# Delta's copies ahead of delta u, a constant row on TensorE, and large transfers in pieces, in a four-layer state-space kernel

## The chip, the cores and the metric

One core of one Trainium2 chip runs the whole program. Its engines are TensorE (PE; PEld is its loading of weights), VectorE (DVE), ScalarE (ACT), GpSimd (POOL) and SyncE (SP). SP issues every DMA here. The metric is the device time of one execution in microseconds (us), lower being better; it is given as the median of three runs, beside one profiled execution.

## The reference

Four layers run on x of 8 x 48 x 48 x 96 numbers; each adds to x a selective scan over a depthwise convolution. Of layers 0 to 2 (B = 8 batches, L = 2304 positions, Din = 192 channels, N = 16 states, K = 4 directions), cut to what matters:

```
xc, z = split(groupnorm(x) @ in_proj_w.T);  xc = silu(depthwise_conv3x3(xc) + conv_b)
xs = stack([x_hw, x_wh, reversed x_hw, reversed x_wh])        # 4 directions
dts, Bs, Cs = split(einsum('bkdl,kcd->bkcl', xs, x_proj_w))   # the projection
delta = softplus(dt_proj_w @ dts + dt_proj_b);  A = -exp(A_logs)
for each position:                                            # the scan
    h = exp(delta * A) * h + (delta * u) * B                  # per channel, per state
    y = sum over states of h * C
y = sum of the 4 directions + D * u
x = x + (layernorm(y) * silu(z)) @ out_proj_w.T
```

Layer 3 writes the scan as decay * cumsum(delta * B * u / (decay + 1e-12)), with decay = exp(cumsum(delta * A)). That decay runs to zero within some positions.

## The kernel before

**Tiling.** The eight batches go through a layer two at a time ("pair"); layers 0 to 2 make 12 pairs. The 192 channels of the pair's two batches are three tiles t of 128 partitions: 128 channels of batch 0, 128 of batch 1, and the 64 left of both. A pair has 12 *groups* (t, phase ph, direction d): ph says along which image axis the positions run, d whether forward or backward. A group has three *chunks* of 768 positions (`SCAN`), and a chunk 16 *units* n. A unit holds two states of 64 channels on its 128 partitions, so 16 units make 16 states of 128 channels. That is 576 units a pair and 6912 in layers 0 to 2.

**One unit** does this. ACT makes the decay exp(delta * A) (`exp`, L764). For ten of the 16 units, PE spreads the rows of B from `brow` into PSUM (`spread_rows`, L667), DVE multiplies with delta u (`scan`, L794) and DVE scans (L798). For the other six, those of `pooled` (L712), DMA brings B already spread (`bb`, L724), POOL multiplies it with delta u ahead of time (`weigh`, L741), and the decay stands in PSUM. POOL then multiplies the scan's h by C (`cb`, loaded spread by DMA; L807), and PE sums over the states (`add_up`, L854) into `acc`, which ACT adds to y (`collect`, L871) at the end of a chunk.

**Order of the work.** `run` (L1170) writes the program's order by hand, one unit after the other, and each engine executes its own instructions in that order. Iteration k issues `get_ready(k + 1)`: loads of C three units ahead, of B four (`LOADS`), `weigh` and the decays two ahead (`DECAYS`), the spread of the next unit. Then comes unit k's scan and the sums of unit k - 2 (`LAG`). So the weighing for unit j stands on POOL just ahead of the product of unit j - 3. Since every DMA goes through SP in this order, a DMA that has to wait on SP for its data or buffer holds the DMAs behind it.

**Side work** is written as generators, and one `yield` is a step. `prepare` (L580) makes delta and delta u for the next chunk, one step a unit, in two halves of 384 positions. `prologue` (L287, the next pair: norm, projection, convolution, the projections xd of dts, B and C) and `epilogue` (L998, the pair before: layer norm, gate, output) get one step a unit between them, shared out by their planned totals of 300 and 195 steps (L1238, L1240).

**Delta** is softplus(v) = relu(v) + log(1 + e), with e = exp(-|v|) and a correction e - ((1 + e) - 1). A half issues three ACT instructions for |v|, relu and e (L611 to L613), three for log, w1 = 1 + e and then 1 - w1 (L615 to L617), and eight fp32 matmuls that add e, w1, log and relu into a PSUM bank v (L623). `to_twins` (L574, L578) then copies v by four ACT instructions of 64 partitions into `dl`, where each half of the channels stands twice. DVE multiplies v by u in place in PSUM (`times_u`, L631 and L634), and four more copies of L578 write delta u into `du`. Banks of `psum` are two, and the side work uses them too.

**Large transfers.** The prologue loads x of a batch whole (864 KB, L366; in layer 0 it stores it, L364), and stores the projection of a phase and batch whole (684 or 864 KB, L492). Four steps after the latter it reads B and C back (`raw`, L437), cuts them into three bf16 parts and stores those as `xb` (L456), from which `brow` is loaded (L749, with the chunk's first C). y of a tile is stored whole (1152 KB, L875), and the epilogue, whose first load is its first step, reads it back as `ey` (L1030).

**Layer 3** (`Edge`, L877) computes the two ends of the 2304 positions alone, 192 each, and tests that the decay has run out; the whole layer runs again under a condition otherwise. Its 48 chunks take the last tenth of the time.

Of the kernel before, what the change touches and what calls it, by code (L numbers as in the profile page):

```python
# [40 lines left out]
BF16 = mybir.dt.bfloat16  # L41
AF = mybir.ActivationFunctionType
# [61 lines left out]
def ss2d_layers_kernel(ctx: ExitStack, tc: tile.TileContext, x_in, consts, weights, out):  # L104
# [55 lines left out]
    nc.vector.tensor_copy(pick, sel[: 2 * NR])  # L160


    twin = cpool.tile([P, 64], F32, name="twin")
    nc.vector.tensor_add(twin, ident[:, 0:64], ident[:, 64:P])

# [14 lines left out]
    nc.vector.tensor_add(centre, ident, off)  # L180
    centre_22 = cpool.tile([P, P], F32, name="centre_22")
    nc.vector.tensor_add(centre_22, ident, off_22)
    minus_group = cpool.tile([DM, DM], F32, name="minus_group")
    nc.scalar.activation(minus_group, group_w, AF.Copy, scale=-1.0)

# [101 lines left out]
    def prologue(l, p, short=False, first=False):  # L287
# [44 lines left out]
        for b in range(2):  # L332
            x = tmp.tile([DM, L], F32, name=f"x_{l}_{p}_{b}", tag="tmp")
            if l == 0:
                loaded = []

                def load(c0, m):
                    ld = sm2.tile([P, 4, DM], F32, name="ld", tag="ld")
                    nc.sync.dma_start(
                        ld[: m // 4],  # L340
                        x_in[2 * p + b, c0 : c0 + m, :].rearrange("(q j) c -> q j c", j=4),
                    )
                    loaded.append(ld)

                load(*CHUNKS[0])
                load(*CHUNKS[1])
                for _ in range(3):
                    yield
                for i, (c0, m) in enumerate(CHUNKS):
                    q, ld = m // 4, loaded[i]  # L350
                    ps = bank()
                    for j in range(4):
                        nc.tensor.transpose(
                            ps[0:DM, j * q : (j + 1) * q], ld[:q, j, :], ident[:q, :q]
                        )
                    yield True
                    nc.scalar.copy(
                        x[:, c0 : c0 + m].rearrange("c (q j) -> c j q", j=4),
                        ps[0:DM, :m].rearrange("c (j q) -> c j q", j=4),
                    )  # L360
                    if i + 2 < NCH:
                        load(*CHUNKS[i + 2])
                    yield
                nc.sync.dma_start(src[b], x)  # L364
            else:
                nc.sync.dma_start(x, src[b])  # L366
            for _ in range(4):
                yield


# [57 lines left out]
        def later(i, held, f, *args):  # L428
            steps.setdefault(i, []).append((held, f, args))
# [37 lines left out]
        def x_projection(i, ph, b):  # L467

            o, got = 15 * i, {}

            def put(ps, c0, m):
                if "xt" not in got:
                    got["xt"] = tmp.tile([ly.nx, L], F32, name=f"xt_{l}_{p}_{ph}_{b}", tag="tmp")
                xt, r0, nr = got["xt"], c0 // W, m // W
                if ph == 0:
                    nc.scalar.copy(xt[:, c0 : c0 + m], ps[: ly.nx, :m])
                else:
                    nc.scalar.copy(
                        xt.rearrange("p (w h) -> p h w", h=H)[:, r0 : r0 + nr, :],
                        ps[: ly.nx, :m].rearrange("p (r w) -> p r w", w=W),  # L480
                    )

            def mul(half, c0, m):
                if half == 0:
                    got["ps"] = bank()
                project(got["ps"], ph, b, half, lambda z: z[:, c0 : c0 + m], slice(0, m))

            for j, (c0, m) in enumerate(CHUNKS):
                later(o + 3 * j, True, mul, 0, c0, m)
                later(o + 3 * j + 1, True, mul, 1, c0, m)  # L490
                later(o + 3 * j + 2, False, lambda *a: put(got["ps"], *a), c0, m)
            later(o + 15, False, lambda: nc.sync.dma_start(xd[ph, b], got["xt"]))  # L492
            row = 2 * ly.rank
            parts_of(
                o + 19, ph, b,
                lambda d: xd[ph, b, row + 2 * NS * d : row + 2 * NS * d + NS, :].rearrange(
                    "n (q m) -> (n q) m", q=4
                ),
                lambda d: xb[ph, b, :, d].rearrange("k n (q m) -> (n q) k m", q=4),
                4 * NS, L // 4,  # L500
            )
# [69 lines left out]
                state[c.l, c.p]["xd"][c.ph, b, c.d * r : (c.d + 1) * r, c.c0 : c.c0 + c.m],  # L571
            )

    def to_twins(z, at, v):  # L574

        for g in range(2):
            for h in range(2):
                nc.scalar.copy(z[64 * h : 64 * h + 64, g, at], v[64 * g : 64 * g + 64])  # L578

    def prepare(c):  # L580
        l, p, t, ph, d = c.l, c.p, c.t, c.ph, c.d
        ly, s = layers[l], state[l, p]
# [10 lines left out]
        for z in range(0, c.m, HALF):  # L593
# [23 lines left out]
            nc.scalar.activation(w1, w1, AF.Identity, bias=ones, scale=-1.0)  # L617
            yield
            v = bank()[:, :m]
            for i, z1 in enumerate((e, w1, lg, x)):  # L620
                for g in range(2):
                    half = slice(64 * g, 64 * g + 64)
                    nc.tensor.matmul(  # L623
                        v[half], ident[:, half], z1, start=(i == 0), stop=(i == 3)
                    )
                if i % 2 == 1:
                    yield

            def times_u(o):
                if ph == 0:  # L630
                    nc.vector.tensor_mul(o, v, u[:, c.c0 + z : c.c0 + z + m])  # L631
                    return
                r0 = (c.c0 + z) // H
                nc.vector.tensor_mul(  # L634
                    o.rearrange("p (w h) -> p w h", h=H),
                    v.rearrange("p (w h) -> p w h", h=H),
                    u[:, r0 : r0 + m // H, :],
                )
# [18 lines left out]
            yield  # L657


    def pieces(m):  # L660
# [8 lines left out]
                start=True, stop=True,  # L669
            )  # L670

    late_act, late_sums = [], []

    def collected():
        some = bool(late_sums)
# [8 lines left out]
    class Chunk:  # L684
# [23 lines left out]

        def pooled(self, n):

            return n in (2, 5, 7, 10, 13, 15) and self.l < NLAYER - 1

# [24 lines left out]
        def weigh(self, n):  # L737

            if self.pooled(n):
                b = self.b[n][:, : self.m]  # L740
                nc.gpsimd.tensor_mul(b, b, self.du[n % 2])  # L741

        def load(self, n):

            s, m, at = state[self.l, self.p], self.m, slice(self.c0, self.c0 + self.m)
            if n == 0:
                self.brow = rpool.tile([2 * NR, SCAN], BF16, name="brow", tag="brow")
                for j, b in enumerate(range(2) if self.t == 2 else (self.t, self.t)):
                    nc.sync.dma_start(  # L749
                        self.brow[NR * j : NR * j + NR, :m],  # L750
                        s["xb"][self.ph, b, :, self.d, :, at],
                    )
            self.cb[n] = cb = cbpool.tile([P, SCAN], F32, name="cb", tag="cb")
            self.fetch(cb, NS, n)

# [107 lines left out]
        def collect(self):  # L863

            l, p, t, s = self.l, self.p, self.t, state[self.l, self.p]
            if self.ph == self.d == 0 and self.first:
                s["y", t] = ypool.tile([P, L], F32, name=f"y_{l}_{p}_{t}", tag="y")
            acc = self.acc[:, :, : self.m // 2]
            if self.ph == 1:
                acc = acc.rearrange("p a (w h) -> p a w h", h=H)  # L870
            nc.scalar.copy(self.y_part(s["y", t]), acc)  # L871
            if self.ph == self.d == 1 and self.last:
                if t == 0:
                    s["yd"] = dram.tile([3, P, L], F32, name=f"yd_{l}_{p}", tag="yd")
                nc.sync.dma_start(s["yd"][t], s["y", t])  # L875

    class Edge:  # L877

# [119 lines left out]
    def epilogue(l, p):  # L998
# [26 lines left out]
        def load(i):  # L1025
# [144 lines left out]
    def run(pairs, short):  # L1170
# [58 lines left out]
        for k, ((l, p, unit), c, n) in enumerate(todo):  # L1229
# [172 lines left out]
```

## Time and profile before

| | |
|---|---|
| three runs | median 20515.53 us, 20514.31 to 20521.39 |
| the profiled execution's own time | 20509.65 us |
| its span, first to last instruction | 20507.7 us |
| TensorE clock granted, mean | 0.904 |
| busy over the span | POOL 87%, DVE 86%, PE 84%, ACT 79% |
| layers 0 to 2, 300 to 18550 us | POOL 16959 us of 18250, DVE 16669, PE 15470, ACT 14655 |
| layer 3, 18550 us to the end | PE 1592 us of 1958, ACT 1446, DVE 895, POOL 720 |
| DMA moved | 4200 MB, 221 GB/s at a busy share of 0.85 in layers 0 to 2 |

How to read it. A row of the groups names a line, an engine, an operation, what it writes and reads, the shape, the count, then busy us, mean ns of one, and the engine's idle time before those instructions with what ended it. A row of the waits says who waited for whom: total us, times, longest. A row of the windows gives a stretch (from:to and its length), then the busy us and the count of instructions for PE, PEld, DVE, ACT and POOL, then the granted clock, the busy share of the DMA engines and GB/s. A row of the timeline has start, length, engine, line, operation, out<-in, and in brackets the idle time before it and what ended that. SPq is SP issuing a DMA, not moving it.

### The profile page before, as it was taken

The numbers are of one execution on the slowest core, as the hardware profiler recorded it, in microseconds if no ns is written. First come the engines' busy times: TensorE is split into PE (matmuls) and PEld (weight loads), VectorE is DVE, ScalarE is ACT, GpSimd is POOL, SyncE is SP. The second block draws the span as 40 slices with busy tenths as digits, with TensorE's granted clock in tenths as the row PEclk, the third lists the DMA queues.
The fourth block names the chain that finished last, engine by engine and source line by source line (L and its number), as shares of the span: only waits on it lengthen the run. The fifth ranks groups of instructions, "written<-read, shape, count | busy, mean of one in ns | idle before, by whom it ended". The sixth has DMA issues, their size and how long they took to land. (4 is left out here: it accounts for less than half of the span.)

```text
span 20507.7 us, 304889 instructions
## 1 busy us (share of the span) xinstructions
PE 17283.2 (84%) x88322; PEld 7546.6 (37%) x88322; DVE 17656.0 (86%) x14161; ACT 16243.7 (79%) x30020; POOL 17768.2 (87%) x10121
## 2 busy tenths in 40 slices
PE   8888888888888888888888888888888888888886
PEld 2323333333333333333333333333333333335565
DVE  5999999999999999999999999989989989995543
ACT  5777887887887887887877887877877877877776
POOL 5999999999999999999999999999999999995432
PEclk8998998998998999998998999988988998999997
DMA  5888888888888888888888888888888888883221
GB/s 147 223 221 222 219 220 224 222 219 221 220 225 222 219 229 221 221 229 219 221 228 220 217 225 219 218 218 220 217 219 219 220 219 222 219 220 109 76 72 51
DMA packets 1963444, 4200.13 MB, mean 205 GB/s; under 512 B 369456, under 2 KB 720048, under 8 KB 1948592
## 3 DMA queue, kind: packets, MB, share of 16 engines
q1 hardware_dynamic: 1961776, 4180.52, 77.8%
q8 instruction: 726, 11.89, 0.3%
q14 instruction: 942, 7.72, 0.2%
HBM read 4026.64 MB, written 152.27 MB: 204 GB/s over the span
## 5 line engine op out<-in xcount | busy, mean ns | idle before, releaser
L807 POOL TENSOR_TENSOR cb<-cb,da 128x768 f32<-128x768 f32 x4320 | 7831.3, 1817 | 799.5 <-issue 258.3
L854 PE MATMUL acc<-cb,twin 128*64 128x384 f32 x27648 | 7018.1, 542 | 663.6 <-POOL cb L807 660.3
L798 DVE TENSOR_TENSOR_SCAN da<-da,carry,b 128x768 f32<-128x768 f32 x2880 | 5223.3, 1814 | 176.4 <-ACT b L764 2.3
L741 POOL TENSOR_TENSOR bb<-bb,du 128x768 f32<-128x768 f32 x2592 | 4714.0, 1819 | 361.0 <-DMA bb<-xd 207.8
L794 DVE TENSOR_TENSOR b<-du,b 128x768 f32<-128x768 f32 x4320 | 4087.6, 946 | 883.9 <-PE b L667 785.4
L807 POOL TENSOR_TENSOR cb<-cb,bb 128x768 f32<-128x768 f32 x2592 | 4705.1, 1815 | 155.0 <-DVE bb L798 57.1
L667 PE MATMUL b<-brow,pick 96*64 96x512 bf16 (+2 forms) x18816 | 2761.6, 355 | 1787.6 <-DVE da L798 1408.4
L764 ACT ACTIVATE da<-dl,a 128x768 f32<-128x768 f32 x4320 | 4013.6, 931 | 245.8 <-POOL cb L807 214.0
L854 PEld LDWEIGHTS acc<-cb,twin 128*64 128x64 f32 x27648 | 2268.9, 150 | 3089.4 <-issue 1400.3
L798 DVE TENSOR_TENSOR_SCAN bb<-b,carry,bb 128x768 f32<-128x768 f32 x1728 | 3109.0, 1799 | 114.8 <-ACT b L764 53.5
L764 ACT ACTIVATE b<-dl,a 128x768 f32<-128x768 f32 x2592 | 2334.4, 901 | 590.2 <-DVE da L798 558.4
L798 DVE TENSOR_TENSOR_SCAN da<-da,b 128x768 f32<-128x768 f32 x1440 | 2525.4, 1754 | 85.6 <-DVE b L794 0.9
L667 PEld LDWEIGHTS <-pick 96*64 96x64 bf16 x18816 | 974.1, 114 | 4192.1 <-DVE da L798 2506.3
L578 ACT COPY dl<-ps 64x384 f32<-64x384 f32 x3456 | 1635.3, 473 | 756.7 <-PE ps L623 720.7
L312 PE MATMUL ps<-pad,diag 128*128 128x480 f32 (+1 forms) x4320 | 2165.7, 599 | 11.5 <-DVE eyc L1087 9.9
L623 PE MATMUL ps<-du,cst 128*64 128x384 f32 (+1 forms) x7296 | 1709.7, 516 | 93.1 <-ACT du L617 77.0
L578 ACT COPY du<-ps 64x384 f32<-64x384 f32 x3456 | 1635.7, 473 | 190.0 <-DVE ps L634 91.2
L798 DVE TENSOR_TENSOR_SCAN bb<-b,bb 128x768 f32<-128x768 f32 x864 | 1502.2, 1739 | 94.9 <-ACT b L764 40.5
L623 PE MATMUL ps<-dl,cst 128*64 128x384 f32 (+1 forms) x7296 | 1412.4, 483 | 0.0
L312 PEld LDWEIGHTS ps<-pad,diag 128*128 128x128 f32 x4320 | 687.5, 191 | 1211.4 <-issue 1090.1
L603 PE MATMUL ps<-dts,w 6*128 6x384 f32 (+5 forms) x2432 | 946.3, 595 | 176.1 <-DMA dts<-xd 103.7
L611 ACT ACTIVATE du<-ps,w 128x384 f32<-128x384 f32 (+1 forms) x912 | 521.4, 572 | 622.3 <-PE ps L603 611.5
(144 smaller groups left out, 19159.8 us busy)
## 6 DMA issues: line engine op xcount, KB each, us to landing
cb<-xd SPq DMA_DIRECT2D x13952, 192.0 KB
bb<-xd SPq DMA_DIRECT2D x5184, 192.0 KB
brow<-xb SPq DMA_DIRECT2D x864, 72.0 KB
yd<-y SPq DMA_DIRECT2D x48, 1152.0 KB
ey<-yd SPq DMA_DIRECT2D x256, 216.0 KB
cb<-xd SPq DMA_DIRECT2D x128, 384.0 KB
ex<-xs SPq DMA_DIRECT2D x256, 108.0 KB
xd<-xt SPq DMA_DIRECT2D x32, 684.0 KB
```

The lines of the kernel that those rows point to most:

```text
L312: nc.tensor.matmul(ps[:, :m], ly.diag[:, int(t == 2), j, :], pad[:, r0 + dy : r0 + dy + nr, dx : dx + W], start=(j == 0), stop=(j == 8),)
L578: nc.scalar.copy(z[64 * h : 64 * h + 64, g, at], v[64 * g : 64 * g + 64])
L603: nc.tensor.matmul(o[:, :m], ly.dtw[q0 : q0 + r, k, chans], dts[q0 : q0 + r, at], start=True, stop=True,)
L611: nc.scalar.activation(e, v, AF.Abs, bias=bias)
L623: nc.tensor.matmul(v[half], ident[:, half], z1, start=(i == 0), stop=(i == 3))
L667: nc.tensor.matmul(o[64 * h : 64 * h + 64], pick[:, b, n : n + 1].to_broadcast([2 * NR, 64]), rows, start=True, stop=True,)
L741: nc.gpsimd.tensor_mul(b, b, self.du[n % 2])
L764: nc.scalar.activation(da, self.dl[n % 2], AF.Exp, scale=layers[self.l].a2[:, int(self.t == 2), n % 2, k, i : i + 1],)
L794: nc.vector.tensor_mul(b, self.du[n % 2], b)
L798: nc.vector.tensor_tensor_scan(way(h), way(da), way(b), start, ALU.mult, ALU.add)
L807: nc.gpsimd.tensor_mul(c, c, h)
L854: nc.tensor.matmul(self.acc[64 * g : 64 * g + 64, a, : self.m // 2], twin, c[:, a, :], start=False, stop=(pair + 2 == NS and not self.turns),)
```

## The change

- **Delta.** 1 - w1 is no longer made on ACT (L617 goes). PE adds the 1 as a bf16 matmul of a constant row (`unit`, `unit_row`) and takes w1 off with the weights `less` = -identity. So a half has ten matmuls, and w1 is added ahead of e.
- **Delta's copies ahead of delta u.** Delta's four copies have a step of their own in both halves. `times_u` follows one step later and writes into `du` in SBUF, and three copies in SBUF replace four out of PSUM. In the second half all of this is one step later than before: delta's copies at unit 12, `times_u` at 13, delta u's copies at 14 of the chunk before.
- **Pooled units** are 2, 4, 7, 9, 12, 15 in place of 2, 5, 7, 10, 13, 15.
- **brow** of the next chunk of the same pair is loaded at unit 6, no longer with that chunk's first C (unit 12).
- **Transfers in pieces.** x goes in five pieces, one a step, with two more steps instead of four behind. The projection is stored in five pieces (phase 0 as each is computed, phase 1 from step 14 on), and `raw` is read at step 24 of a projection instead of step 19 (its whole store was at step 15). y is stored in six pieces of 192 KB, one a unit, but all at once for the pair's last tile. The epilogue waits four steps ahead of its first load.
- The planned totals become 311 and 199 steps.

```diff
+    less = cst[:, P : 2 * P]
+    unit = cpool.tile([P, 64], BF16, name="unit")
+    nc.gpsimd.memset(unit, 0.0)
+    nc.gpsimd.memset(unit[0:1], 1.0)
+    unit_row = cpool.tile([P, 1], BF16, name="unit_row")
+    nc.gpsimd.memset(unit_row, 1.0)
...
+    nc.scalar.activation(less, ident, AF.Copy, scale=-1.0)
...
-                nc.sync.dma_start(src[b], x)
-            else:
-                nc.sync.dma_start(x, src[b])
-            for _ in range(4):
+            for c0, m in CHUNKS:
+                piece = slice(c0, c0 + m)
+                if l == 0:
+                    nc.sync.dma_start(src[b, :, piece], x[:, piece])
+                else:
+                    nc.sync.dma_start(x[:, piece], src[b, :, piece])
+                yield
+            for _ in range(2):
                 yield
...
-            later(o + 15, False, lambda: nc.sync.dma_start(xd[ph, b], got["xt"]))
+            def store(c0, m):
+                nc.sync.dma_start(xd[ph, b, :, c0 : c0 + m], got["xt"][:, c0 : c0 + m])
+
+            for j, (c0, m) in enumerate(CHUNKS):
+                later(o + 3 * j + 3 if ph == 0 else o + 14 + j // 2, False, store, c0, m)
             row = 2 * ly.rank
             parts_of(
-                o + 19, ph, b,
+                o + 24, ph, b,
...
             nc.scalar.activation(w1, e, AF.Identity, bias=ones)
-            nc.scalar.activation(w1, w1, AF.Identity, bias=ones, scale=-1.0)
             yield
             v = bank()[:, :m]
-            for i, z1 in enumerate((e, w1, lg, x)):
+            for g in range(2):
+                nc.tensor.matmul(
+                    v[64 * g : 64 * g + 64], unit, unit_row.to_broadcast([P, m]),
+                    start=True, stop=False,
+                )
+            for w, z1 in ((less, w1), (ident, e), (ident, lg), (ident, x)):
                 for g in range(2):
                     half = slice(64 * g, 64 * g + 64)
-                    nc.tensor.matmul(
-                        v[half], ident[:, half], z1, start=(i == 0), stop=(i == 3)
-                    )
-                if i % 2 == 1:
+                    nc.tensor.matmul(v[half], w[:, half], z1, start=False, stop=(z1 is x))
+                if z1 is e or z1 is x:
                     yield
...
-            to_twins(dl, at, v)
+            for g in range(2):
+                for h in range(2):
+                    nc.scalar.copy(dl[64 * h : 64 * h + 64, g, at], v[64 * g : 64 * g + 64])
             if z + m == c.m:
                 if l == NLAYER - 1:
                     c.sum_up()
                 c.ready = True
+            yield
+            times_u(du[:, 0, at])
+            yield
+            for h in (1, 0):
+                nc.scalar.copy(du[64 * h : 64 * h + 64, 1, at], du[64:P, 0, at])
+            nc.scalar.copy(du[64:P, 0, at], du[0:64, 0, at])
+            if z + m < c.m:
                 yield
-            times_u(v)
-            yield
-            to_twins(du, at, v)
-            yield
...
+    def store_some(n):
+        for _ in range(min(n, len(late_stores))):
+            o, z, at = late_stores.pop(0)
+            nc.sync.dma_start(o[:, at], z[:, at])
...
-            return n in (2, 5, 7, 10, 13, 15) and self.l < NLAYER - 1
+            return n in (2, 4, 7, 9, 12, 15) and self.l < NLAYER - 1
...
-                nc.sync.dma_start(s["yd"][t], s["y", t])
+                for z in range(0, L, SCAN // 2):
+                    late_stores.append((s["yd"][t], s["y", t], slice(z, z + SCAN // 2)))
+                if t == 2:
+                    store_some(NS)
...
+        for _ in range(4):
+            yield
         load(0)
...
+            store_some(1)
             if done:
-                behind, done = Side(epilogue(*done), 195), None
+                behind, done = Side(epilogue(*done), 199), None
             if unit == LAG and following:
-                ahead = Side(begin(*following), 300)
+                ahead = Side(begin(*following), 311)
...
+            if n == 6 and coming_to < len(chunks):
+                z = chunks[coming_to]
+                if (z.l, z.p) == (l, p):
+                    z.load_rows()
```

More of the change, by code (lines that the diff above doesn't have):

```diff
@@ L572, in load_dt @@
             )
[L574 to L578, printed above, removed]
     def prepare(c):
@@ L670, in spread_rows @@
             )
-    late_act, late_sums = [], []
+    late_act, late_sums, late_stores = [], [], []
+    def store_some(n):
+        for _ in range(min(n, len(late_stores))):
+            o, z, at = late_stores.pop(0)
+            nc.sync.dma_start(o[:, at], z[:, at])
     def collected():
@@ L741, in weigh, with load_rows @@
                 nc.gpsimd.tensor_mul(b, b, self.du[n % 2])
+        def load_rows(self):
+            if self.brow is not None:
+                return
+            self.brow = rpool.tile([2 * NR, SCAN], BF16, name="brow", tag="brow")
+            for j, b in enumerate(range(2) if self.t == 2 else (self.t, self.t)):
+                nc.sync.dma_start(
+                    self.brow[NR * j : NR * j + NR, : self.m],
+                    state[self.l, self.p]["xb"][
+                        self.ph, b, :, self.d, :, self.c0 : self.c0 + self.m
+                    ],
+                )
         def load(self, n):
-            s, m, at = state[self.l, self.p], self.m, slice(self.c0, self.c0 + self.m)
             if n == 0:
[L747 to L752, printed above, removed]
+                self.load_rows()
             self.cb[n] = cb = cbpool.tile([P, SCAN], F32, name="cb", tag="cb")
```

## The prediction

> **What bounds the kernel now.** First the engines' totals on the page, then the windows for layers 0 to 2, then windows group by group for one pair (boundaries every 48th POOL product of L807 in the timeline).
>
> ```profile
> PE 17283.2 (84%) x88322; PEld 7546.6 (37%) x88322; DVE 17656.0 (86%) x14161; ACT 16243.7 (79%) x30020; POOL 17768.2 (87%) x10121
> ```
>
> ```profile
> 300.00:18550.00 18250.00, 15469.52 (x77705) 6320.37 (x77705) 16668.67 (x12538) 14655.24 (x27072) 16959.05 (x9627) 0.91 0.85 221
> ```
>
> ```profile
> 7841.10:7974.20 133.10, 102.77 (x544) 45.56 (x544) 118.83 (x94) 107.15 (x202) 118.00 (x71) 0.88 0.82 221
> 7974.20:8095.40 121.20, 106.65 (x552) 42.16 (x552) 115.63 (x88) 97.51 (x186) 117.44 (x67) 0.99 0.89 225
> ...
> 8595.40:8729.00 133.60, 112.43 (x635) 57.72 (x636) 119.24 (x93) 120.57 (x217) 117.88 (x67) 0.89 0.82 211
> 8729.00:8856.10 127.10, 108.04 (x636) 53.59 (x636) 118.29 (x92) 113.45 (x210) 117.68 (x67) 0.91 0.87 222
> 8856.10:8977.10 121.00, 114.92 (x542) 39.36 (x539) 114.84 (x86) 93.22 (x173) 117.30 (x66) 1.00 0.90 231
> ```
>
> No engine stands out by its total. The groups show it: each has the same 117 to 118 us of POOL and about as much DVE, and the second and the last shown, where side work is light, end 3 to 4 us after POOL's busy time. The others last 127 to 134 us. So POOL with DVE is the floor, and what is lost is lost where side work delays one of them. A chunk's sum says the same: POOL 22 x 1.817 = 40.0 us; DVE 10 x (0.946 + 1.794) + 6 x 1.779 + 2 x 0.684 (`times_u`) = 39.4 us. Two engines in balance cannot catch up what either loses.
>
> Who delays them: the waits from 300 to 18600 us, for POOL and for DVE.
>
> ```profile
> POOL bb L741 <- DMA bb<-xd: 187.4, 95, 7.0
> ...
> POOL cb L807 <- DMA bb<-xd: 67.5, 102, 2.7
> POOL cb L807 <- DMA cb<-xd: 61.1, 52, 3.0
> ...
> POOL bb L741 <- DMA cb<-xd: 55.0, 32, 6.1
> ```
>
> ```profile
> DVE b L794 <- PE b L667: 779.9, 741, 5.9
> DVE ps L634 <- ACT dl L578: 116.3, 115, 3.6
> ...
> DVE ps L631 <- ACT dl L578: 85.2, 98, 3.5
> ```
>
> And one stall in the timeline, at a pair's start:
>
> ```profile
> 13977.65 0.36 SPq L875 DMA_DIRECT2D yd<-y  x1
> ...
> 13985.48 0.58 SPq L366 DMA_DIRECT2D x<-xs  x1
> ...
> 13994.92 1.80 POOL L741 TENSOR_TENSOR bb<-bb,du 128x768 f32<-128x768 f32 x1 [5.72 <-DMA bb<-xd]
> ```
>
> Between the first and the last line, 1152 KB of y, 324 KB for the epilogue and 864 KB of x go out beside the loads of C and B. At a DMA share of 0.85 for 221 GB/s, all engines busy would be about 260 GB/s; these 2.4 MB are 9 us of that, with 15% spare, and loads run three to four units (some 8 us) ahead. So POOL waits.
>
> **What the Trainium skill says.** "DMA: Bandwidth & Descriptors", section "Queues, rings and completion order": each DMA engine takes descriptors in ring order, and SP has one ring on each. So a load issued behind a large transfer queues behind it; the 5.72 us above agree. The same page, "Rules for kernel authors", wants 1 MiB per DMA for bandwidth. Here the loads of 192 KB that make most of the traffic already run at 221 GB/s, so I charge the pieces, of the same size, nothing for being small. "VectorE: DVE Perf Modes", section "The TRN2 errata", prices ScalarE at 224 + N cycles of 1.2 GHz out of SBUF, 172 + N out of PSUM: for N = 384, 507 and 463 ns; the 473 ns of L578 out of PSUM agrees, the other stands in no row of before. "FP8 and Floating Point Precision", "TensorE Precision Notes": fp32 takes four passes; the trace shows only the direction: four bf16 matmuls (L667, row below) take 0.52 us for 768 columns twice, four fp32 ones (L854) 0.81 for 384 twice, each count two halves side by side.
>
> **The ceiling.** Over the 12 groups of the pair shown, length is 1519 us and the larger of POOL and DVE sums to 1425: 94 us above the floor. The three light groups (2nd, 6th, 9th) keep 3.1 us each, so 12 x 3.1 = 37 stay. At each pair's boundary PE waits for dts twice (4.3 and 3.7 us, timeline at 7797 and 7841), which the change leaves: 8. Left to gain: 94 - 37 - 8 = 49 us a pair, 588 us for 12.
>
> **Part by part**, for one pair (36 chunks, 72 halves, 1528 us on average):
>
> ```profile
> L578 ACT COPY du<-ps 64x384 f32<-64x384 f32 x3456 | 1635.7, 473 | 190.0 <-DVE ps L634 91.2
> L617 ACT ACTIVATE du<-du,ones 128x384 f32<-128x384 f32 (+1 forms) x912 | 553.2, 607 | 28.5
> ...
> 8010.87 0.52 PE L667 MATMUL b<-brow,pick 96*64 96x512 bf16 x4
> ```
>
> *ACT.* L617 goes: 0.607 us a half. Four copies of 0.473 (1.89 us) become three, between 0.473 (as out of PSUM) and 0.507 (the skill's price): 1.42 to 1.52; I take 1.50. Together 1.0 us a half, 6.0 a group, 72 a pair. ACT has slack where it is 97 of 121 us, so there it is worth nothing; POOL and DVE hide it. In the 7th and 8th groups (120.6 of 133.6, 113.5 of 127.1) and the 1st and 4th (107 of 133, 110 of 130), it comes late to exponentials and copies. I count two thirds of the 6 us in the 7th, half in the 8th, a third in each of the others: 4 + 3 + 2 + 2 = **-11**. Bounds: 0 (other waits take its place) and -24.
>
> *times_u.* It overwrote v, so DVE stood until the four copies had read it: 201 us, 17 a pair. A step later and written elsewhere, it waits for PE's v alone. DVE is in balance with POOL, but has its own slack in most groups: one third, **-6**; bounds 0 and -17. I take its length unchanged: 0.554 us at 384 columns into PSUM against 0.355 at 192 into SBUF (layer 3's rows) fit one line of 0.16 + N x 1.03 ns.
>
> *Transfers.* POOL's four waits above are 371 us, 31 a pair; by groups, counted in the trace, most lie in the 1st, 10th and 11th (y, x; the projection's stores and `raw`). Pieces one or two a step let loads go between, `raw` is issued when its stores have landed, and `brow` leaves a bunch with C and B at unit 12. But the last tile's 1152 KB still goes in one burst. I take 40%: **-12**; bounds 0 and -31. PE's waits for `brow` (177 us) are partly the same stalls and are not counted again. SP gets 39 more issues a pair of about 0.5 us, 20 us in 1528, in its waiting time: 0. Moved past SP's loads are the five steps of `raw` and `xb`, which nothing needs before the next pair. The wait for landed y moves from SP's head by four steps; behind it stand all loads of C and B, so this is a gain or nothing.
>
> *PE.* Two bf16 matmuls over 384 columns cost, at the row above, 0.26 us a half; at fp32 speed 0.40; if they run while PE waits for w1, nothing. A gain is excluded: they only add. I take 0.26 x 72 = 19 us, hidden where PE has slack (it is 115 of 121 us in the 9th group without setting the pace), a fifth on the path through DVE's wait for the spread: **+4**; bounds 0 and +29.
>
> *Pooled units and du's later copies.* Adding up DVE's and POOL's times unit by unit, DVE is latest against POOL at units 1, 6, 9 and 14 with the old list (by 3.6 to 3.7 us), which is where POOL idles before L807 (218, 176, 81, 181 us, counted in the trace); with the new list at 14 alone (3.6, elsewhere at most 2.9). That speaks for a gain; but where DVE is early it now reaches further (1.0 instead of 1.8), and buffers stop it there. du's last copy comes a unit later, and the weighing of unit 2 stands just ahead of product 15. From `times_u` on, ACT needs about 0.9 + 0.9 + 0.2 + 1.5 - 0.6 = 2.9 us (two exponentials, a carry, three copies; the first ones start with scan 13's end); POOL is free for it after scan 14 and product 14, 2.8 + 1.8 = 4.6 us. Behind the copies stand ACT's next exponentials; 1.7 us of margin. I take **0**; bounds -10 and +20.
>
> *Layer 3 and the start.* 48 chunks save one ACT instruction of 192 columns, about 0.3 us of latency: **-12** in all, with a few us at the first projection; bounds 0 and -25.
>
> Sum: 12 x (-11 - 6 - 12 + 4) - 12 = **-312 us**, half of the ceiling. From 20509.65, the profiled execution's own time, that is 20198; the median of the runs is 6 us above it: 20204, rounded to **20205**.
>
> **Rivals.**
> 1. *Little moves.* POOL and DVE stay in step, a removed stall shows as the next one (PE's late spread, already DVE's largest wait), and the last tile's burst stays. For it: one engine's wait has many causes in the wait list. Against: light groups do end near the floor. A quarter of the sum: -80, **20435**.
> 2. *Nearly all goes.* The single late point of the new list lets loaded groups run like light ones: -588 + 28 for PE's share, **19955**. Against: DVE itself is 119 us in the loaded groups.
> 3. *Slower: du is late.* If side work fills the 1.7 us of margin, the weighing of unit 2 waits on ACT, and POOL with it, once a chunk. At 1 us over the margin it costs 432 us against 312 gained: **20635**. It decides from 0.7 us a chunk. Against: weighings waited under 60 us for ACT before, with du a unit earlier.
>
> **Chances.** Forecast 0.60 (20205; own range 20100 to 20340, from the parts' bounds taken half), rival 1 0.21, rival 2 0.10, rival 3 0.09. About 0.2%, 41 us, is what a measurement can tell here: a third of rival 1 lies within it. Faster 0.60 + 0.10 + 0.14 = 0.84, same 0.07, slower 0.09. The range 19950 to 20465 leaves out rival 3, a part of rival 1 and the far end of rival 2: two in ten.
>
> **What would show it.** ACT about 900 us less busy and DVE's waits for `dl` near zero; POOL's DMA waits from 371 to some 220 us; the 7th and 8th groups some 4 us shorter each. Wrong if POOL's `bb` products wait for ACT `du`, or if DVE's wait for the spread grows from 780 us by over 200.

## The result and the profile after

The changed kernel takes **20825.1 us** (median; 20806.2 to 20837.5) against 20515.5: a ratio of 1.015, with a 95% interval of 1.0132 to 1.0167. It is slower by 310 us, where 312 us less were forecast. Its profiled execution took 20806.17 us, with a span of 20804.4.

The engines' totals on the page of the changed kernel:

```profile
PE 17740.5 (85%) x90146; PEld 7707.3 (37%) x90146; DVE 17632.3 (85%) x14161; ACT 15493.2 (74%) x28234; POOL 17779.3 (85%) x10124
```

ACT has lost 750 us of work, POOL and DVE have what they had, PE has 457 us more. Nothing here says where 300 us went: no engine is busy for a clearly larger share of the span than before. The windows for layers 0 to 2 of the changed kernel (from:to, length; then busy us of PE, PEld, DVE, ACT and POOL, granted clock, DMA share, GB/s) say as little:

```profile
300.00:18850.00 18550.00, 15915.74 (x79199) 6471.99 (x79195) 16579.58 (x12488) 13902.43 (x25294) 16915.60 (x9594) 0.88 0.86 217
```

Nearly the same work of DVE and POOL fills a stretch 300 us longer, so the added time is idle time on both: DVE's idle time there rose from 1581 to 1970 us (the stretch less the busy time), POOL's from 1291 to 1634. So the waits are the view to read. DVE's, from 300 to 18850 us (who waited for whom: total us, times, longest us):

```profile
DVE b L822 <- PE b L683: 1441.6, 918, 9.8
DVE b L822 <- PE acc L882: 121.5, 65, 4.8
DVE bb L826 <- ACT b L792: 90.9, 84, 3.5
```

L822 is what L794 was, L683 what L667 was. DVE's wait for the spread has gone from 780 to 1442 us. The two rows of 201 us for delta's copies are gone: one is left with 2 us. POOL's waits, from 300 to 18900 us, in the same form:

```profile
POOL bb L762 <- DMA bb<-xd: 244.0, 220, 5.5
POOL cb L835 <- PE acc L882: 138.3, 95, 4.3
POOL cb L835 <- DMA bb<-xd: 125.7, 157, 2.6
POOL cb L835 <- DMA cb<-xd: 111.0, 119, 2.2
POOL cb L835 <- PE b L683: 101.7, 58, 3.7
POOL bb L762 <- DMA cb<-xd: 49.1, 54, 2.9
...
POOL bb L762 <- ACT du L671: 21.6, 15, 2.4
```

The four DMA rows add up to 530 us, 371 before, though the transfers were cut to help them. Du's last copy (L671), feared late, holds the weighing up for 22 us in this window.

Which units wait is not in these rows, since all units share a line. Counting DVE's idle time ahead of L822 by unit in the trace: 725 us at unit 5, 170 at 10, 325 at 13, where the kernel before has no spread at all (its list pools those three). In exchange the 301 us that it waits at unit 11 fell to 13, and 82 at unit 6 to nothing. A stall at unit 5, from the timeline of the changed kernel (start, length, engine, line, operation; in brackets the idle time before it and what ended that):

```profile
3989.53 0.33 PE L629 MATMUL ps<-unit_row,unit 128*64 128x384 bf16 x2
...
3990.58 1.81 DVE L826 TENSOR_TENSOR_SCAN da<-da,carry,b 128x768 f32<-128x768 f32 x1
...
3990.99 1.46 PE L636 MATMUL ps<-dl,cst 128*64 128x384 f32 x8
...
3992.30 1.79 DVE L826 TENSOR_TENSOR_SCAN bb<-b,carry,bb 128x768 f32<-128x768 f32 x1
3992.37 1.07 PE L319 MATMUL ps<-pad,diag 128*128 128x480 f32 x2
...
3993.38 1.51 PE L867 MATMUL acc<-y,cst 128*64 128x384 f32 x8
...
3994.72 0.81 PE L882 MATMUL acc<-cb,twin 128*64 128x384 f32 x4
...
3995.36 0.50 PE L683 MATMUL b<-brow,pick 96*64 96x512 bf16 x4
...
3995.90 0.96 DVE L822 TENSOR_TENSOR b<-du,b 128x768 f32<-128x768 f32 x1 [1.80 <-PE b L683]
```

The spread (L683) needs the PSUM buffer of unit 3, whose scan (the row at 3990.58) ended at 3992.39; it starts at 3995.36. Until then PE works off what stands ahead of it: the end of delta's matmuls, a convolution matmul of the side work, then the four fp32 matmuls of `begin_sum` (L867), which bring the old y into `acc`, and the two of `add_up` (L882), all issued ahead of the spread. (The trace keeps one fp32 matmul as two records: `add_up` issues two a unit, 13824 in 6912 units, and the trace has 27648. So the x8 of L867 are four matmuls.) The Trainium skill, "PSUM — Partial Sum Buffer", section "Engine vs sequencer instructions", says that matmuls start and complete in program order; this stretch agrees. Nor can the spread be issued early: it has two PSUM buffers, and PE already stood at it for DVE's scan, 2054 us in all from 300 to 18850 us.

**The theory** from here on: PE's program order, with the pooled list. What iteration k puts on PE stands ahead of the spread of unit k + 2 and delays it. `begin_sum` and delta's last matmuls stand ahead of spread 5, delta's second half ahead of spreads 12 and 13. The old list pools 5 and 13, so no spread is needed there; the new list asks for one, and asks for it right behind a pooled unit (4 and 12), which keeps DVE for one scan of 1.8 us instead of a product and a scan of 2.7. **The rival** (P): the list itself is worse, through loads, GpSimd and ScalarE, whatever PE does. A second rival is the added row, which puts more on PE.

### The profile page after: what moved, and what is told of

Its sections match the earlier page's. It is cut to its first block, busy times and chain, and to the rows that moved or that the text cites. A ratio compares the mean times of both kernels' runs of the same rounds, so it can differ in the third digit from the quotient of the medians.

```text
span 20804.4 us, 306916 instructions
## 1 busy us (share of the span) xinstructions
PE 17740.5 (85%) x90146; PEld 7707.3 (37%) x90146; DVE 17632.3 (85%) x14161; ACT 15493.2 (74%) x28234; POOL 17779.3 (85%) x10124
## 4 chain that ended last, share of the span: by engine, by line
PE 36%; DVE 21%; DMA 7%; ACT 6%; issue 5%; POOL 1%; SPq 1%; DVEq 0%; POOLq 0%; ACTq 0%
DVE da L826 11%; PE acc L882 9%; PE ps L636 6%; DVE b L822 6%; PE ps L319 5%; PE b L683 4%; DMA cb<-xd 3%; PE acc L867 2%; PE ps L612 2%; DMA bb<-xd 2%; DVE bb L826 1%; PE ps L476 1%; PE ps L1043 1%; SPq L745 1%; PE acc L1000 1%
## 5 line engine op out<-in xcount | busy, mean ns | idle before, releaser
L882 PE MATMUL acc<-cb,twin 128*64 128x384 f32 x27648 | 7105.4, 560 | 263.3 <-POOL cb L835 257.8
L822 DVE TENSOR_TENSOR b<-du,b 128x768 f32<-128x768 f32 x4320 | 4100.7, 949 | 1603.2 <-PE b L683 1464.5
L683 PE MATMUL b<-brow,pick 96*64 96x256 bf16 (+2 forms) x18816 | 2783.3, 364 | 2204.0 <-DVE da L826 2082.1
L882 PEld LDWEIGHTS acc<-cb,twin 128*64 128x64 f32 x27648 | 2217.4, 154 | 2551.2 <-issue 1393.8
L683 PEld LDWEIGHTS <-pick 96*64 96x64 bf16 x18816 | 972.3, 117 | 4734.7 <-DVE da L826 3087.7
L319 PE MATMUL ps<-pad,diag 128*128 128x480 f32 (+1 forms) x4320 | 2215.6, 611 | 19.9 <-DVE du L642 9.7
L636 PE MATMUL ps<-dl,cst 128*64 128x384 f32 (+1 forms) x7296 | 1501.2, 488 | 0.0
L636 PE MATMUL ps<-du,cst 128*64 128x384 f32 (+1 forms) x7296 | 1378.3, 494 | 63.8 <-ACT du L625 63.8
L612 PE MATMUL ps<-dts,w 6*128 6x384 f32 (+5 forms) x2432 | 1111.2, 694 | 139.0 <-DMA dts<-xd 138.1
L670 ACT COPY du<-du 64x384 f32<-64x384 f32 x1728 | 882.7, 511 | 21.9
```

Of the source, the lines that this page charges most:

```text
L319: nc.tensor.matmul(ps[:, :m], ly.diag[:, int(t == 2), j, :], pad[:, r0 + dy : r0 + dy + nr, dx : dx + W], start=(j == 0), stop=(j == 8),)
L612: nc.tensor.matmul(o[:, :m], ly.dtw[q0 : q0 + r, k, chans], dts[q0 : q0 + r, at], start=True, stop=True,)
L636: nc.tensor.matmul(v[half], w[:, half], z1, start=False, stop=(z1 is x))
L670: nc.scalar.copy(du[64 * h : 64 * h + 64, 1, at], du[64:P, 0, at])
L683: nc.tensor.matmul(o[64 * h : 64 * h + 64], pick[:, b, n : n + 1].to_broadcast([2 * NR, 64]), rows, start=True, stop=True,)
L822: nc.vector.tensor_mul(b, self.du[n % 2], b)
```

## The experiments

Each kernel was timed beside the kernel before; the latter's medians in these comparisons lie between 20496 and 20516 us, so differences between kernels of different comparisons are good to some 20 us. "By unit" means DVE's idle time ahead of the `b` product, counted in the trace from 300 us on.

### One part taken out, one part alone

In the changed kernel, the list alone put back (e1), and the row alone put back (e2: 1 - w1 on ACT again). Then each part alone in the kernel before: list (e3), row (e4), transfers with `brow` at unit 6 (e5), and the copies' new order (e6).

```diff
-            return n in (2, 4, 7, 9, 12, 15) and self.l < NLAYER - 1
+            return n in (2, 5, 7, 10, 13, 15) and self.l < NLAYER - 1
```

```diff
             nc.scalar.activation(w1, e, AF.Identity, bias=ones)
+            nc.scalar.activation(w1, w1, AF.Identity, bias=ones, scale=-1.0)
...
-            for g in range(2):
-                nc.tensor.matmul(
-                    v[64 * g : 64 * g + 64], unit, unit_row.to_broadcast([P, m]),
-                    start=True, stop=False,
-                )
...
```

> The changed kernel with the old list of pooled units (2, 5, 7, 10, 13, 15). Theory L (the list): with the new list units 5 and 13 are spread by TensorE; unit 5's spread stands behind the eight matmuls that bring the old y into acc, unit 13's behind delta's matmuls, and VectorE comes for them after a pooled unit of 1.8 us instead of 2.8 us. Then VectorE's wait for the spread falls from 1445 us to below 900 us and the time to 20250 to 20450 us. Theory R (the constant row): TensorE has too much to do with ten matmuls a half; the time stays above 20650 us and the wait above 1200 us.

> The changed kernel with 1 - w1 made on ScalarE again and eight fp32 matmuls a half, no constant row. Theory L: the wait of unit 5 stays, the time is 20700 to 20850 us. Theory R: TensorE is relieved by 0.3 us a half, VectorE's wait for the spread falls below 1000 us and the time to 20250 to 20450 us, with the granted clock back above 0.895.

> The kernel before with the new list of pooled units (2, 4, 7, 9, 12, 15) alone. Theory L: VectorE's wait for the spread rises from 780 us to over 1300 us, most of it ahead of units 5 and 13, and the time to 20850 to 21100 us (what the other three parts save is missing). Theory R: within 60 us of 20515 us, or faster, as the sums of VectorE and GpSimd by unit had it.

> The kernel before with the constant row alone: one ScalarE instruction less a half, two bf16 matmuls more. Theory L: 20440 to 20540 us, the wait for the spread stays below 900 us. Theory R: 20700 us or more, wait above 1200 us, granted clock below 0.89.

> The kernel before with the transfers alone (pieces, later raw and first epilogue load, brow at unit 6, late stores of y). The old list with the other three parts is 421 us faster than before, the row alone 56 us slower, so copies and transfers together are worth some 480 us if they add up. Theory T (transfers carry most of it): 20150 to 20250 us, GpSimd's waits for DMA below 250 us. Theory C (the copies carry most of it): 20350 to 20460 us.

> The kernel before with delta's copies ahead of delta u alone (a step of their own, times_u into SBUF, three copies). Theory T: 20380 to 20480 us. Theory C: 20100 to 20250 us; in both, VectorE's waits for delta's copies (201 us in layers 0 to 2) go to near zero.

| kernel | us | ratio to before, 95% |
|---|---|---|
| e1, changed with the old list | 20087.8 | 0.9795 (0.9779 to 0.9811) |
| e2, changed without the row | 20740.5 | 1.0112 (1.0095 to 1.0129) |
| e3, list alone | 20775.0 | 1.013 (1.0113 to 1.0147) |
| e4, row alone | 20565.2 | 1.0028 (1.0018 to 1.0038) |
| e5, transfers alone | 20295.9 | 0.9892 (0.9874 to 0.9911) |
| e6, copies alone | 20222.3 | 0.9862 (0.9845 to 0.9878) |

So the list is the loss: 20825 - 20088 = 737 us beside the other parts, 266 alone. All else together is worth -421 us (e1), and nearly adds up: alone, row +56, transfers -215, copies -289, together -448. Not every expectation came true. e1 gained some 160 us more than the best expected; e4 lies 25 us above its range; e5 came between its two theories, e6 where the copies' theory had it; e3 lost less than expected, and its wait for the spread is 888 us where over 1300 were expected. e1's windows and DVE wait (same columns as above):

```profile
300.00:18130.00 17830.00, 15544.27 (x79166) 6250.88 (x79164) 16547.39 (x12484) 13820.06 (x25288) 16882.38 (x9590) 0.93 0.89 225
```

```profile
DVE b L822 <- PE b L683: 784.0, 646, 11.1
```

Nearly the same instructions as in the changed kernel, in 720 us less. DVE's wait for the spread is half as long; by unit, nothing at 5 and 13, and 27 us at 11.

The list alone does less harm in the kernel before, and by another wait. The waits of e3, whole run (L631 and L634 are `times_u`, L667 the spread):

```profile
DVE b L794 <- PE b L667: 888.3, 743, 6.4
...
DVE ps L631 <- ACT dl L578: 356.2, 197, 103.8
DVE ps L634 <- ACT dl L578: 291.7, 219, 4.4
```

There `times_u` waits for delta's copies: inside layers 0 to 2 these two rows come to 540 us, 201 before, while unit 5 waits only 184. In the changed kernel the copies' new order takes that wait away, and unit 5 waits 725. It looks as if the same stall moved on, and as if the list therefore cost more beside the new order; this is read from the numbers and was not tried. In e6, with the old list, `times_u` no longer shows among the larger waits of layers 0 to 2, and its copies take 511 ns, where the prediction took 507 from the Trainium skill ("VectorE: DVE Perf Modes", section "The TRN2 errata"):

```profile
L653 ACT COPY du<-du 64x384 f32<-64x384 f32 x1728 | 882.8, 511 | 29.2
```

### What of PE's queue it is

e7 splits `begin_sum`: two of its four matmuls at n = 1, two at n = 2 (the expectation counts records, eight and four). e8 pools 5 again in place of 4, and keeps 9 and 12. e11 takes out the step between the halves, so that delta's second half, its matmuls and its copies and `times_u` with them, comes where it came before the change.

```diff
-            if n == 1:
-                self.begin_sum()
+            if n in (1, 2):
+                self.begin_sum(n - 1)
```

```diff
-            return n in (2, 4, 7, 9, 12, 15) and self.l < NLAYER - 1
+            return n in (2, 5, 7, 9, 12, 15) and self.l < NLAYER - 1
```

```diff
-            if z + m < c.m:
-                yield
```

> The changed kernel, new list, with the eight matmuls that bring the old y into acc issued as four with the sum of unit 1 and four with that of unit 2. Theory S (these eight, just ahead of unit 5's spread, are what VectorE waits for after the short unit 4): the wait ahead of unit 5 falls from 725 us to below 350 us and the time to 20450 to 20650 us. Rival W (after a pooled unit TensorE has 1 us less whatever stands in its queue): the wait falls by less than 150 us and the time stays above 20750 us.

> The changed kernel with the list 2, 5, 7, 9, 12, 15: unit 5 pooled again in place of 4, units 9 and 12 as in the new list. Theory S: unit 5 makes most of the loss, 20150 to 20350 us. Rival W: units 10 and 13, which follow pooled ones where delta's second half is on TensorE, make as much: 20450 to 20650 us.

> The changed kernel, new list, without the step between the two halves of delta: the second half's matmuls are issued at iterations 9 and 10 instead of 10 and 11, its copies, times_u and delta u's copies one unit earlier. Theory Q (what TensorE is given at iteration j delays the spread of unit j + 2, which costs nothing where that unit is pooled): unit 12 is pooled in this list, so VectorE's wait ahead of unit 13 falls from 325 us to below 150 us, the time by 100 to 250 us. Rival P (the product of unit 14 is late by the sums of VectorE and GpSimd themselves, 349 us of GpSimd's idle time there): the wait ahead of 13 only moves, the time stays within 60 us of 20825 us.

| kernel | us | ratio to before, 95% | DVE by unit: 5 | 10 | 11 | 13 |
|---|---|---|---|---|---|---|
| changed | 20825.1 | 1.015 (1.0132 to 1.0167) | 725 | 170 | 13 | 325 |
| e7 | 20591.1 | 1.0034 (1.0021 to 1.0046) | 417 | 130 | 13 | 427 |
| e8 | 20459.8 | 0.9971 (0.996 to 0.9981) | pooled | 67 | 20 | 608 |
| e11 | 20656.1 | 1.0063 (1.0048 to 1.0079) | 743 | 12 | 206 | 22 |

Each edit moves the unit that the theory names. Two fp32 matmuls fewer ahead of spread 5 take 308 us off its wait (to 417, where below 350 was expected) and 234 us off the time. Pooling 5 takes 365 us off the time. With the second half a step earlier, the waits at 10 and 13 go from 495 to 34 us, 193 us come back at 11, and 169 us are gained. e8 also shows the limit, and its time lies where its rival had put it: unit 5 makes about half of the loss. With PE's stall at 5 gone, 608 us gather at 13, and POOL waits for its own loads (whole run, 248 in the changed kernel):

```profile
POOL bb L762 <- DMA bb<-xd: 381.2, 325, 5.7
```

### The rows loaded early

e12 leaves out the load of `brow` at unit 6, so that it comes with the first C again.

```diff
-            if n == 6 and coming_to < len(chunks):
-                z = chunks[coming_to]
-                if (z.l, z.p) == (l, p):
-                    z.load_rows()
```

> The changed kernel, new list, with brow loaded together with the chunk's first C (unit 12) as before, not at unit 6. Theory B (at unit 6 the brow load stands just ahead of the B of pooled unit 12, which GpSimd then waits for): GpSimd's wait ahead of weighing unit 12 falls from 215 us to below 60 us, that ahead of unit 2 rises, and the time falls by 50 to 200 us. Rival: the two waits change places and the time stays within 50 us of 20825 us.

20852.3 us, 1.0166 (1.015 to 1.0181): 27 us more than the changed kernel, and the intervals overlap. POOL's idle time ahead of the weighing of 12 falls from 215 to 19 us, and ahead of the weighing of 2 it rises from 41 to 234. The two waits change places, as the rival had it; this part is worth next to nothing.

### The best of both

e9 is e1 with the split `begin_sum`; e10 is e9 without the row.

> The changed kernel with the old list and the old y brought into acc in halves. The old list alone gave 20088 us. If those eight matmuls in one piece still cost something at unit 6 (200 us of VectorE's wait for the spread there), the time is 19950 to 20050 us; if the pooled unit 5 already covers them, 20060 to 20110 us.

> The same without the constant row (1 - w1 on ScalarE). The row alone cost 56 us, and taking it out of the changed kernel gained 84 us; if that adds up, 60 to 90 us faster than with the row in the same comparison. If the row's saving on ScalarE counts now that less else stands in the way, within 20 us of it or slower.

e9: 20100.2 us, 0.9797 (0.9784 to 0.9811), the same as e1. Splitting gains 234 us under the new list and nothing under the old one, as the theory has it: the delay costs where a spread is due behind it. e10: **20005.0 us**, 0.975 (0.9737 to 0.9763), faster than the kernel before by 510 us and than the changed one by 820. Leaving out the row is worth 95 us here, and 84 in e2. The totals of e9, then of e10, and e10's wait, whole run:

```profile
PE 17366.2 (86%) x90146; PEld 7486.6 (37%) x90146; DVE 17611.7 (88%) x14161; ACT 15408.0 (77%) x28234; POOL 17752.1 (88%) x10124
PE 17289.7 (86%) x88322; PEld 7397.6 (37%) x88322; DVE 17611.2 (88%) x14161; ACT 15923.1 (80%) x29150; POOL 17762.6 (89%) x10121
```

```profile
DVE b L813 <- PE b L674: 729.5, 607, 11.3
```

Without the row ACT carries 515 us more than in e9 and PE only 77 us less, and that is still the better trade. It fits a queue of PE that others wait for, but which wait the row lengthens was not tried. (Against the changed kernel PE has 451 us less, but 374 of these lie already between the changed kernel and e9, which have the same 90146 records.)

### Does the theory carry the whole loss?

If PE's order were all, the new list with every relief should come near e10. e13 is the changed kernel without the row, with `begin_sum` split and the second half a step earlier. e14 is e10 with the second half a step earlier, to price that step under the old list.

> The changed kernel, new list, with the old y in halves, the second half of delta a step earlier and no constant row. If the three add up: 20825 - 234 - 169 - 84 = 20338 us. Theory K (TensorE's collisions are all of the list's cost): within 60 us of the old list's 20005 us. Rival P (the list itself is worse): 20280 us or more, with GpSimd idle ahead of products 5, 8, 11 and 14 though VectorE's wait for the spread is below 900 us.

> The old list with the old y in halves, no constant row, and the second half of delta a step earlier (its matmuls at iterations 9 and 10, where the kernel before had them, against 10 and 11). Theory Q: unit 12 is spread in the old list and unit 13 is not, so the earlier step puts matmuls ahead of a spread that is needed: VectorE's wait ahead of units 11 and 12 rises from 95 us to over 200 us and the time from 20005 us to 20060 to 20180 us. If the step doesn't matter there: within 40 us of 20005 us.

| kernel | us | ratio to before, 95% | DVE by unit |
|---|---|---|---|
| e13 | 20357.3 | 0.9924 (0.9908 to 0.9941) | 353 at 5, 193 at 11, 30 at 13 |
| e14 | 20198.5 | 0.9855 (0.9838 to 0.9873) | 154 at 6, 187 at 11, 93 at 12 |
| e10 | 20005.0 | 0.975 (0.9737 to 0.9763) | 177 at 6, 27 at 11, 68 at 12 |

The three reliefs add up: 20825 - 234 - 169 - 84 = 20338, measured 20357. But that is 352 us above e10, so PE's order as it was relieved here is not all of the list's cost. Of the three reliefs the row is no part of that cost, since leaving it out is worth as much under the old list. Without the row the list costs 735 us (e2 against e10, which also splits `begin_sum`, worth nothing there by e9). The other two edits give back 383 of them (e2 to e13), and 352 stay. Rival P had put e13 at 20280 us or more, and there it came. Of P's two signs one shows: POOL idles ahead of products 5, 8, 11 and 14 (486 us together, 106 in e10). The other does not: DVE's wait for the spread (whole run) is not below 900 us:

```profile
DVE b L811 <- PE b L672: 971.9, 785, 11.7
```

Even relieved, the new list still waits 353 us at unit 5, and POOL 262 us for the weighing of 12 (93 for that of 13 in e10). How much of the 352 us is PE's remaining queue at 5, and how much loads and POOL, these runs don't part.

e13 and e14 differ in the list alone. There it costs 159 us (20357 - 20198), about a fifth of the 737. So the list has no price of its own: its cost depends on what stands ahead of which spread.

e14 shows how tightly list and order belong together. The very same edit gains 169 us under the new list (e11) and costs 193 under the old one, 18 more than expected at the most: a step later, delta's second half stands ahead of spread 13, which the old list does not need and the new one does. Earlier it stands ahead of 11 and 12, and under the old list the waits there rise from 95 to 280 us.

## Why the prediction was wrong, step by step

**The bound.** Right as far as it went: POOL and DVE are in balance, and what is lost is lost where another engine delays one of them. But the light groups' pace was read as a property of side work alone, and the list of pooled units, which decides which delays matter, was treated as a property of DVE and POOL alone.

**The failed step: pooled units and du's later copies, taken at 0 with -10 to +20 us a pair.** It measured +737 us for the list beside the other parts, 61 a pair, three times the upper bound. The step added DVE's and POOL's times unit by unit and found a single late point at unit 14. PE was no term in that sum, though the prediction's own wait list named it as what DVE waits for longest. A pooled unit is a unit without a spread, so the list also says where PE may be late; the old list had its free units at 5 and 13, whose spreads would stand behind `begin_sum` and delta's matmuls. What the sum promised for POOL did come: its idle time ahead of products 1, 6 and 9 fell from 220, 179 and 85 us to 87, 4 and 0. But ahead of products 5, 8 and 14 it grew, from 104, 30 and 184 us to 282, 169 and 350, and in all it rose by 343 us. The prediction's own alarm, "DVE's wait for the spread grows from 780 us by over 200", went off, at 662. In place of the balance of DVE and POOL the runs show the spread on PE: DVE waits 725 us at unit 5 and 325 at 13, and less of PE's work ahead of these two spreads gives back 383 of the list's 735 us (e2 to e13). What makes the other 352 is open.

The other half of that step was mis-sized too, since even its sign depends on the list: under the old list, delta's and du's second half a step later gains 193 us, 16 a pair (e14 against e10), and under the new one it costs 169 (e11).

**ACT, -11 a pair, and times_u, -6.** The mechanism held: DVE's waits for `dl` fell from 201 to 2 us, and ACT lost 750 us of work. By rows it is 864, L617's 553 and 311 for the copies (three at 511 ns, just above the range taken, in place of four at 473); ACT's busy time counts overlapping instructions once. As times, the parts came out unlike the split. The copies alone, with `times_u` and the later second half, gained 289 us, where their shares (12 x (0.4 x 11 + 6), since the copies were 0.4 of the 1.0 us a half) came to 125. The later second half, worth 193 us under the old list (e14), would cover the rest; the copies without it were not run.

**PE, +4 a pair.** The prediction's price of fp32, 0.40 us, is misread: the four fp32 records of L854 that take 0.81 us are two matmuls, so a pair over 384 columns takes 0.81 us at fp32 against 0.26 at bf16, and the upper bound built on 0.40 was too low. The row takes 0.36 us a half (the group's 330 us over 912 halves), above the 0.26 taken and less than half of the fp32 pair:

```profile
L629 PE MATMUL ps<-unit_row,unit 128*64 128x384 bf16 (+1 forms) x1824 | 330.1, 338 | 0.5 <-ACT ex L1135 0.3 <-DVE du L642 0.2
```

PE's busy total, where overlapping instructions count once, rises by less: 94 us when the row comes alone (e4), 77 from e10 to e9, 58 from e2 to the changed kernel. So most of PE's 457 us more came with the list and not with the row. Together with L617, which goes for the row, the forecast had 12 x (4 - 0.6 x 11) = -31 us; measured are +56 (e4), +84 (e2) and +95 (e10 against e9). No run removes L617 without adding the row, so two readings stay open: L617 was worth nothing and the row costs what a sixth to three tenths of its 330 us on the path would give, or both are larger. Either way the 0.6 us of ACT a half bought nothing that the row on PE did not take back.

**Transfers, -12 a pair.** Right in kind and undersized: -215 us alone, 18 a pair. POOL's four DMA rows fell from 392 us to 268 in e5 (whole run), which is less than the time gained. e5 holds the pieces, the later `raw`, the epilogue's later first load and the earlier `brow` together, and which of them gains was not tried. In the changed kernel the rows rose to 534, with the list as the cause and not the pieces: with the old list beside everything else (e1) they stand at 357.

**Layer 3, -12.** From the last product of layers 0 to 2 to the end: 1943.5 us before, 1883.6 after. -60 us; e5 alone has 37 of them (1906.1), and the row with its saved ACT instruction 9 to 24 (e4 against before, e9 against e10), so it is the transfers more than ACT.

**The rivals.** The third, du late, fell: the weighing waited 22 us for L671. The profile puts a further 103 us of POOL's idle time, ahead of product 14, down to du's copies; in e1, where the copies stand at the same units, that is 19, and e1 takes 20088 us. Its sign was right, its mechanism was not. The slower case that came true, the spread, was named only as a stall that might show next and as a sign to look for, and given no price. With the old list, the other parts made 20088 us, 117 better than the forecast for the whole.

## What to carry to other kernels

When work is shared out by a list of which unit goes which way, lay **every** engine's queue beside the list, including the engine that the listed units skip: a slot in which an engine is not needed may be what hides its heaviest burst. Before moving such a slot, count what stands in program order ahead of the first consumer that now needs it, and how many buffers let the producer run ahead. Try each part of a bundle with the rest held: here three parts were worth 421 us together, and the fourth lost 737.

## What the runs showed of the hardware

The mean granted TensorE clock went, on the whole, with the kernel's time and not with its number of matmuls: 0.924 in e1 with 90146 records of them, 0.876 in e2 with 88322, 0.904 before with as many as e2. It is no strict order: e10 is faster than e1 at 0.918. The Trainium skill, "TensorE: Matmul & The Clock Gate", section "Part 1: The HAM clock gate (the "warmup" mystery)", says that the clock is gated down when the array has been idle; that is in keeping with stalls lowering it, but whether the lower clock is a consequence of the lost time or a part of its cause was not tried. It does show in the matmuls: one of the 27648 `add_up` records took 560 ns on average in the changed kernel (clock 0.88) against 529 in e1. Their median is 486 ns in both, so what differs is how many ran long.

The constant row's bf16 pair over 384 columns took 0.36 us, against 0.26 worked out from the spread's bf16 matmuls and 0.81 for an fp32 pair. What makes the difference, its broadcast operand, its weights or its place between fp32 matmuls, was not tried.
